# Two decoder stages share TensorE: where the media key and value projections stand, how the first statistics are issued, and how the media sums begin

## The chip, the cores and the metric

The kernel runs on one core of a Trainium2 chip. A core has a TensorE for matrix products (its weight loads are shown apart in the profile, as PEld), a VectorE (DVE), a ScalarE (ACT) and a GpSimd (POOL), which run their own queues in order and wait for each other by semaphores. SyncE (SP) issues most of the transfers, which sixteen DMA engines carry out. Matrix products land in PSUM, which VectorE, ScalarE and others empty.

The metric is the device time of one launch in microseconds (us). One execution of the kernel was taken with the hardware profiler; the trace and the page of profile come from it.

## The reference, cut to what matters

A decoder of two layers works on `x`, 8 rows of 512 tokens with 256 channels, in six residual stages, each behind a layer norm. The change touches the fourth and the fifth, `L1_attn` and `L1_xattn`.

The fourth is an attention in integers. Each `quant_act` needs the largest magnitude of its whole tensor before the first value can be rounded:

```python
def quant_act(x, bit):
    n = 2 ** (bit - 1) - 1
    s = jnp.max(jnp.abs(x)) / n
    xq = jnp.clip(ste_round(x / s), -n - 1, n)
    return (xq * s, s)
...
aw = jnp.einsum('ntd,nsd->nts', q, k)
aw, aws = quant_act(aw, 8)
probs, ps = int_softmax(aw, aws, 8)
probs, ps = quant_act(probs, 8)
attn = jnp.einsum('nts,nsd->ntd', probs, v)
attn, as_ = quant_act(attn, 8)
attn = attn.transpose(1, 0, 2).reshape(T, B, E)
out, _ = quant_linear(attn, as_, wo, bo)
```

It has 16 heads of 16 channels and attends over the batch of 8, at each of the 512 positions. So its matrices are small, and many of them are laid out together.

The fifth attends from `x` to a second input, the context or media (`ctx`, also 8 x 512 x 256). Its keys and values depend on the context and a weight alone, and not on anything that the earlier stages compute:

```python
q = xn @ Wq * scale
kv = media @ Wkv
k, v = jnp.split(kv, 2, axis=-1)
...
sim = jnp.einsum('bhid,bhjd->bhij', q, k)
sim = jnp.where(media_mask[:, None, None, :], sim, neg_inf)
attn = jax.nn.softmax(sim, axis=-1)
out = jnp.einsum('bhij,bhjd->bhid', attn, v)
return out @ Wout
```

Here `xn` is `x` behind two layer norms, and there are 8 heads of 64 channels. A mixture of experts (`L1_ffn`) follows and ends the program.

## The kernel before, in words

The class `FastDecoder` keeps `x` in SBUF as 32 tiles of 128 tokens and runs the stages one after the other. A layer on top of the language places the instructions on the queues: each engine's order follows the order of the program, corrected by priorities. `tc.high_priority(AT_ONCE)` moves what is issued under it ahead of other work that is ready; `tc.issue_after(i)` keeps it behind an instruction `i`; `newest(engine)` is the last instruction issued so far for an engine.

**The media keys and values** are computed ahead, wherever TensorE has room in the integer attention. `keys_values` (L2742) takes rows of the context; for each it makes eight *groups*, four of the keys and four of the values. A group is two fp32 products of 128 x 512 (L2773, two records each in the trace, so four records), one copy from PSUM by ScalarE into one of three `kv_o` tiles (L2778), and one transfer of 256 KB to DRAM on SP (L2779). The media stage later loads `ma_kT` and `ma_v` from there (1 MB each, L2860).

**The integer attention** (`stage_quantized_attention`, L2404) runs through five pools of tiles:

- qa1 quantizes `x` and computes queries, keys and values; row 0 of the media keys and values is made here.
- qa2 computes the scores (TensorE, L2590 and L2596) and reduces them (VectorE).
- qa3 is the integer softmax (L2784), nearly all VectorE. Beside it `keys_values` makes rows 1 to 5. Their five contexts are loaded at once into `room`, a tile of the tag `qa_big` with room for eight.
- qa4 is the loop over the values, `for n in range(9)`. `spread(n)` copies the values of step n into a tile with zeros between the heads, two of four copies on GpSimd and two on VectorE (L2631, 1.15 us each). `turn(n)` rounds the probabilities (VectorE), widens them with four ScalarE operations (L2641), transposes them in two halves on TensorE (L2649), and copies each half out on VectorE (L2652). `weigh(n - 1)` does the products (L2662), one ScalarE copy into `m_[:, n - 1]` (L2670) and one VectorE reduction for the largest magnitude (L2671). After each step two groups of rows 6 and 7 follow, 16 in all, from a generator: `keys_values(range(6, B), None, "tr", 4)`. With `room` None, the context of each row has the tile `kv_ctx`, of which there is one buffer. The groups take their PSUM from the same four `tr` buffers as the transposes. `m_`, 8 x 1024 values on each partition, is a new tile of the tag `qa_big`.
- Behind the loop the magnitudes are reduced to one number over all partitions, and a few one-column VectorE operations make the scales. `bias_parts` (L2383) splits the output bias into three bf16 pieces with ten VectorE operations, and one more scales a row (`orow`).
- qa5 rounds `m_` in eight pieces (ScalarE L2709, then VectorE L2710), transposes them (TensorE, L2713) and copies the result out through a helper that shares the copies between VectorE and ScalarE (L101, L103). Then, for each of the 8 rows of x, the output product (L2726, L2729) fills one of two PSUM buffers `pj`, VectorE multiplies it by the scale (L2731), and the sum is added to `x` (L2733), on GpSimd for rows 2, 4 and 6 and on VectorE otherwise. After row 0, `twice_normal` (L3014) computes the statistics that the media stage's first row needs: four `bn_stats`, and small operations on 128 x 4 values, most in two reciprocal square roots of ten operations each (L1477 to L1481).

**The media stage** (`stage_media_attention`, L2835) loads keys and values of a row, normalizes it, and works through eight steps for each row: scores of two key tiles (L2901, two PSUM buffers), two exponentials on ScalarE (L2907, into four buffers `ma_e`), the products with the values (L2925), and a running sum of the four exponentials of each pair of heads. The sum begins with a copy of the first exponential by GpSimd (L2912); the three others are added by VectorE (L2914). The softmax is divided by these sums at the end.

Of the kernel before, what the change touches and what calls it, by code (L numbers as in the profile page):

```python
# [27 lines left out]
F32 = mybir.dt.float32  # L28
# [6 lines left out]
ALU = mybir.AluOpType  # L35
# [4 lines left out]
P = 128  # L40
B, S, C = 8, 512, 256
NST = S // P
# [1235 lines left out]
class FastDecoder(Decoder):  # L1278
# [1125 lines left out]
    def stage_quantized_attention(self, w):  # L2404
        nc, q = self.nc, self.q
        wT, ident, ones, magic = q["wT"], q["ident"], q["ones"], q["magic"]
        tc = self.tc
        with tc.tile_pool(reuse_waits="tile", name="qa", bufs=1) as pool:
# [195 lines left out]
            with tc.tile_pool(reuse_waits="tile", name="qa3", bufs=2) as tmp, tc.tile_pool(  # L2604
                reuse_waits="tile", name="qp3", bufs=4, space=PSUM
            ) as psum:
                ptop = self.integer_softmax(tmp, aw, qs, atop)
                room = self.alloc(pool, [P, 8, 2, S], F32, "qa_big")
                for _ in self.keys_values(tmp, psum, range(1, 6), room, "kv", 4):
                    pass  # L2610

                ps_, _ = self.scaled(pool, ptop, 1.0 / 128.0 / 127.0, "qa_ps")
                pr = one("qa_pr")
                nc.vector.reciprocal(pr, ptop)
                nc.vector.tensor_scalar(pr, pr, 127.0, None, ALU.mult)


            m_ = self.alloc(pool, [P, 8, 4, C], F32, "qa_big")
            mtops = one("qa_mtops", 8)

            vz = h16("vz").rearrange("p (j i m a r d) -> p j i m a r d", j=2, i=NST, m=4, a=4, r=4)
# [1 line left out]
            with tc.tile_pool(reuse_waits="tile", name="qa4", bufs=2) as tmp, tc.tile_pool(  # L2623
# [48 lines left out]
                        mtops[:, n : n + 1], m_[:, n], AX.XY, ALU.max, apply_absolute_value=True  # L2672
                    )

                ahead = self.keys_values(tmp, psum, range(6, B), None, "tr", 4)
                for n in range(9):
                    if n < 8:
                        spread(n)
                        turn(n)
                    if n:  # L2680
                        weigh(n - 1)
                    for _ in range(2):
                        next(ahead, None)


            mtop = one("qa_mpart")
            nc.vector.tensor_reduce(mtop, mtops, AX.X, ALU.max)
# [7 lines left out]
            nc.vector.reciprocal(osc_inv, osc)  # L2695
            mT = h16("mT").rearrange("p (c i t m) -> p c i t m", c=2, i=NST, t=B)
            brow = self.alloc(pool, [P, C], BF16, "qa_orow")
            self.bias_parts(brow, q["rb"][:, 3 * C :], osc_inv, "qa_b")
            with tc.tile_pool(reuse_waits="tile", name="qa5", bufs=2) as tmp, tc.tile_pool(
                reuse_waits="tile", name="qp5", bufs=1, space=PSUM  # L2700
            ) as psum:
                orow = self.alloc(tmp, [P, C], F32, "qa_orow_s", bufs=1)
                nc.vector.tensor_scalar(orow, q["wsc"][:, C:], osc, None, ALU.mult)
                for n in range(0, 8, 2):
                    ps = [self.alloc(psum, [P, 8, P], BF16, "tr", bufs=4) for c in range(2)]
                    for h in range(2):
                        f = m_[:, n + h]
                        mi = self.alloc(tmp, [P, 4, C], BF16, "qa_mi")
                        nc.scalar.activation(f, f, AF.Identity, bias=magic[:, 0:1], scale=mr)  # L2709
                        nc.vector.tensor_scalar(mi, f, -MAGIC, None, ALU.add)  # L2710
                        for c in range(2):
                            for m in range(4):
                                nc.tensor.transpose(  # L2713
                                    ps[c][:, 4 * h + m], mi[:, m, c * P : (c + 1) * P], ident
                                )
                    for c in range(2):
                        for st in range(NST):
                            self.evac(
                                mT[:, c, st, :, 16 * n : 16 * n + 32].rearrange("p t (m k) -> p t m k", k=4),
                                ps[c][:, :, 32 * st : 32 * st + 32].rearrange("p m (k t) -> p t m k", t=B),  # L2720
                            )
                for b in range(B):
                    ps = self.alloc(psum, [P, NST, C], F32, "pj", bufs=2)
                    for st in range(NST):
                        for c in range(2):
                            nc.tensor.matmul(  # L2726
                                ps[:, st], mT[:, c, st, b], wT[:, c, 3 * C :], start=(c == 0), stop=False
                            )
                        nc.tensor.matmul(ps[:, st], ones[:, :P], brow, start=False, stop=True)  # L2729
                    o = self.alloc(tmp, [P, NST, C], F32, "qa_o")  # L2730
                    nc.vector.tensor_tensor(o, ps, orow.unsqueeze(1).broadcast_to([P, NST, C]), ALU.mult)  # L2731
                    x = self.x[:, b * NST : (b + 1) * NST, :]
                    (nc.gpsimd if b in (2, 4, 6) else nc.vector).tensor_tensor(x, x, o, ALU.add)  # L2733
                    if b == 0:
                        self.media_stats = {b: self.twice_normal(tmp, b, self.const)}
        self.integers.close()

    def load_media_attention(self):
        self.w_media = super().load_media_attention()
        return self.w_media  # L2740

    def keys_values(self, pool, psum, rows, room, tag, bufs, outs=None):  # L2742

# [91 lines left out]
    def stage_media_attention(self, w, out):  # L2835


        nc, t = self.nc, self.t
        wq, wkv, wo = w
        later = Background()  # L2840
        with self.tc.tile_pool(reuse_waits="tile", name="ma", bufs=2) as pool, self.tc.tile_pool(
# [50 lines left out]
            def scores(n):  # L2892
# [12 lines left out]
                for kt, ps in zip(kts, both):  # L2905
# [1 line left out]
                    nc.scalar.activation(  # L2907
                        ex, ps, AF.Exp, bias=bias[:, b * NST + kt : b * NST + kt + 1], scale=0.125
                    )
                    if kt == 0:  # L2910
                        d["sum", c] = self.alloc(pool, [P, 2, 512], F32, "ma_esum", bufs=3)
                        nc.gpsimd.tensor_copy(d["sum", c], ex)  # L2912
                    else:
                        nc.vector.tensor_tensor(d["sum", c], d["sum", c], ex, ALU.add)  # L2914

            def weigh(n):
                b, rest = divmod(n, 8)
# [622 lines left out]
```

## Time and profile before

| | |
|---|---|
| three runs | 3056.48, 3062.92 and 3061.24 us; median 3061.24 us |
| profiled execution | 3056.84 us, its span in the trace 3054.9 us |
| granted TensorE clock, mean over the span | 0.970 of full speed |
| TensorE | busy 2839.3 us, 93% of the span |
| VectorE | busy 2063.4 us, 68% |
| ScalarE | busy 1192.1 us, 39% |
| GpSimd | busy 428.7 us, 14% |

The trace says where the stages of interest lie (us from the start of the span; busy times from the table of windows over these stretches):

| stage | from, to | TensorE busy | VectorE busy | ScalarE busy | granted clock |
|---|---|---|---|---|---|
| scores and before | 2110 to 2190 | 62.6 of 80 | 59.5 | 24.8 | 0.87 |
| integer softmax, rows 1 to 5 of keys and values | 2190 to 2258 | 61.3 of 68 | 65.4 | 35.9 | 0.97 |
| values loop, rows 6 and 7 | 2258 to 2311 | 45.5 of 53 | 34.8 | 37.5 | 0.91 |
| largest magnitude, rounding, transposes | 2311 to 2329.5 | 10.9 of 18.5 | 15.0 | 14.1 | 0.54 |
| output, first media statistics | 2329.5 to 2353.7 | 11.7 of 24.2 | 23.2 | 0.0 | 0.77 |
| media attention | 2353.7 to 2790 | 421.7 of 436.3 | 313.6 | 174.2 | 0.98 |
| experts, to the end | 2790 to 3054.9 | 237.3 of 264.9 | 36.8 | 40.8 | 0.93 |

How to read what follows: a row of the table of windows gives a stretch of time and what each engine was busy in it, with the number of instructions in brackets. A row of the timeline gives the start, the length, the engine, the line, the operation, the tiles it writes and reads and their shapes, and in square brackets how long the engine had been idle before it and what ended that wait. "x8" at the end of a row means that eight neighbouring records are merged into one. An engine's idle time costs nothing where another engine sets the pace.

### The profile page before, as it was taken

The numbers are of one execution on the slowest core, as the hardware profiler recorded it, in microseconds if no ns is written. First come the engines' busy times: TensorE is split into PE (matmuls) and PEld (weight loads), VectorE is DVE, ScalarE is ACT, GpSimd is POOL, SyncE is SP. The second block draws the span as 40 slices with busy tenths as digits, with TensorE's granted clock in tenths as the row PEclk, the third lists the DMA queues.
The fourth block names the chain that finished last, engine by engine and source line by source line (L and its number), as shares of the span: only waits on it lengthen the run. The fifth ranks groups of instructions, "written<-read, shape, count | busy, mean of one in ns | idle before, by whom it ended". The sixth has DMA issues, their size and how long they took to land. (4 is left out here: it accounts for less than half of the span.)

```text
span 3054.9 us, 39805 instructions
## 1 busy us (share of the span) xinstructions
PE 2839.3 (93%) x14929; PEld 1513.9 (50%) x14944; DVE 2063.4 (68%) x4546; ACT 1192.1 (39%) x1687; POOL 428.7 (14%) x389
## 2 busy tenths in 40 slices
PE   8999999979999999999999999999786999997998
PEld 5653333225555556555555556555344344444665
DVE  7458999977776784356776788548788876764110
ACT  2237776744444421134445421115363444441111
POOL 1111111100011010000011011112111123331111
PEclk9999999988999999999999999999897999997999
DMA  7001212101000011001000012010332132314231
GB/s 245 1 35 51 70 51 68 38 14 57 16 22 22 16 31 36 1 1 43 16 22 22 16 46 69 14 42 28 122 123 82 43 105 76 112 50 104 101 139 62
DMA packets 130695, 168.72 MB, mean 55 GB/s; under 512 B 51761, under 2 KB 79666, under 8 KB 128443
## 3 DMA queue, kind: packets, MB, share of 16 engines
q1 hardware_dynamic: 126394, 154.48, 15.9%
q0 software_dynamic: 4096, 11.59, 1.0%
q8 instruction: 119, 1.95, 0.3%
q14 instruction: 86, 0.70, 0.1%
HBM read 113.12 MB, written 47.50 MB: 53 GB/s over the span
## 5 line engine op out<-in xcount | busy, mean ns | idle before, releaser
L1889 PE MATMUL pj<-w,la_hT 128*128 128x512 f32 x720 | 333.3, 603 | 5.2 <-ACT la_qkT L1942 4.5
L1736 DVE TENSOR_TENSOR x_e<-x_e,x_share 128x1024 f32<-128x1024 f32 x256 | 315.8, 1276 | 14.3 <-ACT x_e L1735 14.2
L1735 ACT ACTIVATE x_e<-sc 128x1024 f32<-128x1024 f32 x256 | 249.3, 1023 | 82.9 <-PE sc L1724 82.9
L1889 PEld LDWEIGHTS pj<-w,la_hT 128*128 128x128 f32 x720 | 132.2, 191 | 152.7 <-issue 113.7
L2016 DVE TENSOR_TENSOR la_e<-sc,la_mask 128x1024 f32<-128x1024 f32 (+1 forms) x128 | 135.3, 1083 | 103.8 <-PE sc L2007 103.8
L3283 POOL TENSOR_TENSOR la_oT<-la_o,x_wide 128x512 f32<-128x512 f32 x64 | 97.9, 1541 | 753.0 <-DMA x_wide<-invs 647.9
L2907 ACT ACTIVATE ma_e<-sc,ma_bias 128x1024 f32<-128x1024 f32 x128 | 135.6, 1110 | 147.3 <-PE sc L2901 145.8
L2233 ACT ACTIVATE lf_gate<-pj,lf_b 128x512 f32<-128x512 f32 (+1 forms) x82 | 56.3, 687 | 334.5 <-PE pj L2212 322.6
L2020 ACT ACTIVATE la_e<-la_e 128x1024 f32<-128x1024 f32 (+1 forms) x128 | 117.5, 946 | 151.8 <-DVE la_e L2016 150.7
L2212 PE MATMUL pj<-lf_hnT,w 128*128 128x512 f32 (+1 forms) x368 | 171.3, 593 | 2.8 <-DVE lf_hid L2238 2.8
L1752 PE MATMUL po<-x_e,x_v 128*32 128x512 f32 x1024 | 139.8, 618 | 34.1 <-DVE x_e L1736 30.1
L2914 DVE TENSOR_TENSOR ma_esum<-ma_esum,ma_e 128x1024 f32<-128x1024 f32 x96 | 120.6, 1260 | 58.8 <-ACT ma_e L2907 30.0
L2212 PE MATMUL sc<-lf_hnT,w 128*128 128x512 f32 x336 | 157.7, 592 | 0.0
L1724 PE MATMUL sc<-x_q,x_k 32*128 32x512 f32 x1024 | 152.5, 645 | 1.7 <-DVE sa_ok L1448 1.4
L2284 PE MATMUL po<-w,lf_hid 128*128 128x256 f32 x640 | 149.0, 379 | 0.0
L2238 DVE SCALAR_TENSOR_TENSOR lf_hid<-sc,lf_b,lf_gate 128x512 f32<-128x512 f32 x70 | 52.4, 748 | 136.9 <-PE sc L2212 133.8
L2027 PE MATMUL po<-la_e,la_v 128*64 128x256 f32 (+1 forms) x1024 | 125.2, 369 | 6.7 <-ACT la_o L2044 6.0
L2007 PE MATMUL sc<-la_qkT 64*128 64x256 f32 (+1 forms) x1024 | 128.9, 375 | 1.1 <-DVE la_e L2016 0.6
L2284 PEld LDWEIGHTS po<-w,lf_hid 128*128 128x128 f32 x640 | 117.8, 190 | 21.2 <-issue 7.4
L2901 PE MATMUL sc<-ma_qT,ma_kT 64*128 64x512 f32 x512 | 127.3, 615 | 0.4 <-ACT ma_e L2907 0.4
L2925 PE MATMUL po<-ma_e,ma_v 128*64 128x512 f32 x512 | 125.2, 610 | 0.0
L2070 PE MATMUL pj<-w,la_oT 128*128 128x256 f32 x512 | 121.0, 383 | 2.0 <-DVE lf_t L1480 0.7
(493 smaller groups left out, 5206.8 us busy)
## 6 DMA issues: line engine op xcount, KB each, us to landing
x_wide<-invs SPq DMA_DIRECT2D x184, 128.0 KB
w<-in_f_w_dram SPq DMA_DIRECT2D x16, 1024.0 KB
kv<-kv_o SPq DMA_DIRECT2D x56, 256.0 KB
slots<-x_empty SPq DMA_DIRECT2D x8, 1028.0 KB
x_mask<-in_x_maskT_dram SPq DMA_DIRECT2D x8, 1024.0 KB
ma_kT<-kv SPq DMA_DIRECT2D x8, 1024.0 KB
ma_v<-kv SPq DMA_DIRECT2D x8, 1024.0 KB
ex_rows<-slots SPq DMA_DIRECT2D x7, 1028.0 KB
```

The costliest lines, as they stand in the source:

```text
L1724: nc.tensor.matmul(pair[r // 2][:, r % 2, :], d["k"][rows, g, kt * P : (kt + 1) * P], d["q"][rows, e, g, :], start=True, stop=True,)
L1735: nc.scalar.activation(ex, d["e"][rest][p], AF.Exp)
L1736: nc.vector.tensor_tensor(ex, ex, d["share"][:, kt, :].unsqueeze(1).broadcast_to([P, 2, 512]), ALU.mult)
L1752: nc.tensor.matmul(d["po"][32 * r : 32 * r + 32, :], d["v"][:, kt, 8 * g + 2 * r + e, :], ex[r // 2][:, r % 2, :], start=(kt == 0), stop=( ...
L1889: nc.tensor.matmul(ps, d["hT"][:, k, i * P : (i + 1) * P], wqkv[:, k, j * S : (j + 1) * S], start=(k == 0), stop=(k == 1),)
L2007: nc.tensor.matmul(both[half][:, r, jj * 256 : jj * 256 + to - j * P], d["qkT"][rows, 4 + c, j * P : (j + 1) * P], d["qkT"][rows, c, j * P ...
L2016: nc.vector.tensor_tensor(ex[:, :, :n_cols], ps[:, :, :n_cols], mask[:, :n_cols].unsqueeze(1).broadcast_to([P, 2, n_cols]), ALU.add,)
L2027: nc.tensor.matmul(out[:, j * P : to], lhsT(j), ex[:, jj * 256 : jj * 256 + to - j * P], start=(j == 0), stop=(j == 3), skip_group_check=True,
L2212: nc.tensor.matmul(ps[:m, :], w1[:, k, at : at + m], held[b]["hnT"][:, k, :], start=(k == 0), stop=(k == 1))
L2284: nc.tensor.matmul(ps[:, :C], held[b]["hid"][:, f, i * P : (i + 1) * P], w2[:, f, :], start=(f == 0), stop=False,)
L2901: nc.tensor.matmul(both[m // 2][:, r, :], d["k"][rows, c, kt * P : (kt + 1) * P], d["q"][rows, c, :], start=True, stop=True,)
L2907: nc.scalar.activation(ex, ps, AF.Exp, bias=bias[:, b * NST + kt : b * NST + kt + 1], scale=0.125)
```

## The change

It has four parts.

1. **The 16 groups of rows 6 and 7 are spread.** `context` loads one context and `keys_values_group` makes one group; `project(tmp, psum, tag, count)` takes the next `count` groups from a list. Three are issued in the softmax, behind the forty of rows 1 to 5. In the values loop one follows each step except where n % 4 is 3, that is seven, and two more behind the loop. One is issued behind each output product until the list is empty, which takes the last four (rows 0 to 3 of x). The context of row 6 now has a place in `room`; that of row 7 has a tile of its own in a new pool `qx`. `m_` is no longer a new tile but a view of `room`.
2. **The bias rows are moved**: `bias_parts` and the scaling of `orow` are issued behind the second pair of rounded pieces (n == 2) and no longer ahead of the first.
3. **The first media statistics are unbroken**: they are issued at the highest priority, and the product and the sum of every row of x after the first (`o` and `x`) are kept behind their last VectorE instruction.
4. **The media sums begin as a sum of two**: nothing is done for the first exponential (kt == 0); the second step adds the first two exponentials into the sum's tile. The GpSimd copies are gone.

In the changed kernel each engine's queue is then ordered as follows where it differs. On TensorE one group stands ahead of a step's transposes in the loop, three behind the last weighing, and in the output two half groups and then whole ones alternate with the products of rows 0 to 3. On ScalarE three `kv_o` copies stand ahead of the first widening, and two stand between the first copies of the rounding. On VectorE the statistics follow the first row of x without a gap. On SP the context of row 7 stands behind three `kv_o` writes, and the loads of `ma_kT` and `ma_v` for the first media row behind the last write.

```diff
                 for _ in self.keys_values(tmp, psum, range(1, 6), room, "kv", 4):
                     pass
 
+                ctx6 = self.context(room[:, 5], 6)
+                groups = [(ctx6, 6, j, g) for j in range(2) for g in range(NST)]
+
+                def project(tmp, psum, tag, count=1):
+                    for group in groups[:count]:
+                        self.keys_values_group(tmp, psum, *group, tag, 4)
+                    del groups[:count]
+
+                project(tmp, psum, "kv", 3)
...
-            m_ = self.alloc(pool, [P, 8, 4, C], F32, "qa_big")
+            m_ = room.rearrange("p n a s -> p n (a s)").rearrange("p n (m c) -> p n m c", c=C)
+            stay = ExitStack()
+            late = stay.enter_context(tc.tile_pool(reuse_waits="tile", name="qx", bufs=1))
+            ctx7 = self.context(self.alloc(late, [P, 2, S], F32, "qa_ctx"), 7)
+            groups += [(ctx7, 7, j, g) for j in range(2) for g in range(NST)]
...
-                ahead = self.keys_values(tmp, psum, range(6, B), None, "tr", 4)
                 for n in range(9):
                     if n < 8:
                         spread(n)
                         turn(n)
                     if n:
                         weigh(n - 1)
-                    for _ in range(2):
-                        next(ahead, None)
-
+                    if n % 4 != 3:
+                        project(tmp, psum, "tr")
+                project(tmp, psum, "tr", 2)
...
-            self.bias_parts(brow, q["rb"][:, 3 * C :], osc_inv, "qa_b")
...
-                nc.vector.tensor_scalar(orow, q["wsc"][:, C:], osc, None, ALU.mult)
...
+                    if n == 2:
+                        self.bias_parts(brow, q["rb"][:, 3 * C :], osc_inv, "qa_b")
+                        nc.vector.tensor_scalar(orow, q["wsc"][:, C:], osc, None, ALU.mult)
                 for b in range(B):
...
+                    project(tmp, psum, "tr")
                     o = self.alloc(tmp, [P, NST, C], F32, "qa_o")
-                    nc.vector.tensor_tensor(o, ps, orow.unsqueeze(1).broadcast_to([P, NST, C]), ALU.mult)
                     x = self.x[:, b * NST : (b + 1) * NST, :]
-                    (nc.gpsimd if b in (2, 4, 6) else nc.vector).tensor_tensor(x, x, o, ALU.add)
+                    with self.tc.issue_after(ahead) if b else nullcontext():
+                        nc.vector.tensor_tensor(o, ps, orow.unsqueeze(1).broadcast_to([P, NST, C]), ALU.mult)
+                        (nc.gpsimd if b in (2, 4, 6) else nc.vector).tensor_tensor(x, x, o, ALU.add)
                     if b == 0:
-                        self.media_stats = {b: self.twice_normal(tmp, b, self.const)}
+                        with self.tc.high_priority(self.AT_ONCE):
+                            self.media_stats = {b: self.twice_normal(tmp, b, self.const)}
+                        ahead = self.newest(mybir.EngineType.DVE)
+            stay.close()
...
+    def context(self, out, b):
+        self.nc.sync.dma_start(
+            out, self.t["ctxT"].rearrange("(k p) n -> p k n", p=P)[:, :, b * S : (b + 1) * S]
+        )
+        return out
+
+    def keys_values_group(self, pool, psum, ctxT, b, j, g, tag, bufs):
+        nc, wkv = self.nc, self.w_media[1]
+        ps = self.alloc(psum, [P, 1, S], F32, tag, bufs=bufs)
+        at = slice(g * P, (g + 1) * P)
+        for k in range(2):
+            w, x = wkv[:, k, j * S : (j + 1) * S], ctxT[:, k, :]
+            w, x = (w[:, at], x) if j == 0 else (x[:, at], w)
+            nc.tensor.matmul(ps[:, 0], w, x, start=(k == 0), stop=(k == 1))
+        o = self.alloc(pool, [P, 1, S], F32, "kv_o", bufs=3)
+        nc.scalar.copy(o, ps)
+        nc.sync.dma_start(self.kv[b, j][:, g * S : (g + 1) * S], o.rearrange("p a n -> p (a n)"))
...
-                    if kt == 0:
+                    if kt == 1:
                         d["sum", c] = self.alloc(pool, [P, 2, 512], F32, "ma_esum", bufs=3)
-                        nc.gpsimd.tensor_copy(d["sum", c], ex)
-                    else:
-                        nc.vector.tensor_tensor(d["sum", c], d["sum", c], ex, ALU.add)
+                    if kt:
+                        nc.vector.tensor_tensor(d["sum", c], d[4 * c] if kt == 1 else d["sum", c], ex, ALU.add)
```

## The prediction, made before the changed kernel ran

> **What bounds the kernel now.** I read the page first (TensorE busy 93% of a 3054.9 us span), then found where the changed lines run, and read the table of windows from 2258 us on; in each row the numbers are length, busy time of TensorE, its weight loads, VectorE, ScalarE and GpSimd, granted TensorE clock, DMA share and GB/s:
>
> ```profile
> 2258.00:2310.00 52.00, 45.53 (x704) 25.93 (x704) 34.41 (x38) 37.52 (x54) 12.89 (x12) 0.91 0.27 93
> 2310.00:2330.00 20.00, 11.43 (x87) 9.01 (x88) 15.85 (x43) 14.14 (x24) 0.35 (x1) 0.57 0.42 159
> 2330.00:2350.00 20.00, 11.19 (x75) 8.46 (x73) 19.64 (x30) 0.00 (x0) 8.05 (x5) 0.81 0.16 52
> 2368.00:2468.00 100.00, 97.72 (x424) 37.62 (x420) 78.37 (x242) 46.56 (x51) 20.38 (x17) 1.00 0.20 65
> ```
>
> So there are four stages with four limits. The values loop (first row) is TensorE's: 45.5 of 52 us. Rounding the values (second) is shared by VectorE and ScalarE. The output (third) is VectorE's, 19.6 of 20. Media attention (fourth) is TensorE's again. Next came the timeline of VectorE in the values loop (start, length, line, idle time before it and its releaser):
>
> ```profile
> 2266.48 1.29 DVE L2652 COPY qa_pT<-tr 128x1024 bf16<-128x1024 bf16 x2 [4.80 <-PE tr L2649]
> 2267.80 2.31 DVE L2631 COPY qa_h<-qa_h 32x1024 bf16<-32x1024 bf16 x2
> 2270.14 1.22 DVE L2671 TENSOR_REDUCE qa_mtops<-qa_big 128x1 f32<-128x1024 f32 x1
> 2271.62 1.29 DVE L2652 COPY qa_pT<-tr 128x1024 bf16<-128x1024 bf16 x2 [0.27 <-PE tr L2649]
> ...
> 2292.51 1.29 DVE L2652 COPY qa_pT<-tr 128x1024 bf16<-128x1024 bf16 x2 [5.65 <-PE tr L2649]
> ...
> 2308.92 1.22 DVE L2671 TENSOR_REDUCE qa_mtops<-qa_big 128x1 f32<-128x1024 f32 x1 [3.03 <-ACT qa_big L2670]
> ```
>
> The period is 5.14 us (2266.48 to 2271.62), and VectorE fills 4.87 of it: it is only 0.27 behind TensorE. The other idle pieces are large: 4.80, 5.65, 0.86 and 3.03. TensorE's own timeline says why:
>
> ```profile
> 2259.06 1.89 PE L2649 MATMUL tr<-qw_ident,qa_wide 128*128 128x128 bf16 x16 [7.73 <-ACT qa_wide L2641]
> 2260.74 5.26 PE L2773 MATMUL tr<-kv_ctx,w 128*128 128x512 f32 x8
> ...
> 2272.58 3.70 PE L2773 MATMUL tr<-w,kv_ctx 128*128 128x512 f32 x8
> ...
> 2286.65 5.37 PE L2773 MATMUL tr<-kv_ctx,w 128*128 128x512 f32 x8 [3.20 <-DMA kv_ctx<-in_ctxT_dram]
> ```
>
> Two projection groups are 8 records: 3.43 us from start to start when warm. They take 5.26 after 7.73 us of idleness, and 5.37 after the 3.20 us wait for a context that has one buffer.
>
> **Projections spread (16 groups of rows 6 and 7).** The work is the same: per group 4 matmul records (1.72 us warm), one ScalarE copy (0.58) and one 256 KB write on SP. Before, all 16 stood in the values loop; now 3 stand in the softmax, 9 in the loop (3 of them behind its last weighing), 4 in the output.
>
> *Softmax, 3 groups.* The 40 groups there end at 2251.3 and TensorE idles to 2259.06, so 5.15 us fit, to 2256.5. But their copies stand before the first widening on ScalarE's queue: the third ends near 2256.5 + 0.06 + 0.58 = 2257.14, where the widening started at 2256.08. Loss 1.06. TensorE's gap shrinks to 2260.12 - 2256.5 = 3.6 us. A gap of 3.20 cooled it above, so I take a cold start again. Row 6's context load joins five at 2175.67, last in the queue: 0 (up to 0.5).
>
> *Loop start.* Cold transposes 1.89, then one group instead of two: cold to about 4.8 us after the restart, as before, so it ends near 2265.1. Transposes 1.0 and weighing 0.6 follow, and the first spread copy (2267.80) starts near 2267.1: gain 0.7, 1.06 already taken off. A warm start would give 2.7.
>
> *Six full turns.* TensorE now needs 1.0 + 0.6 + 1.72 = 3.3, ScalarE 4 x 0.74 + 0.99 + 0.58 = 4.5, VectorE 1.29 + 2.31 + 1.22 = 4.82, with gaps 4.88. VectorE is next: six turns are 29.3, two last reductions 2.44, the last weighing and its copy 0.7. That is 32.4, against 2310.14 - 2267.80 = 42.3. Gain 9.9. The context wait goes, since row 7 has its own tile, loaded near 2257.8 behind three writes on SP and read some 30 us later.
>
> *The clock.* The thinned loop leaves gaps of 1.5 us in a turn with a group, 3.2 in the two without. The trace's nearest row is the scores stage (L2590), also limited by VectorE:
>
> ```profile
> 2160.00:2165.00 5.00, 2.98 (x151) 1.66 (x140) 3.70 (x3) 0.00 (x0) 1.46 (x1) 1.00 0.24 53
> 2165.00:2170.00 5.00, 2.89 (x156) 1.63 (x157) 3.92 (x3) 0.00 (x0) 5.00 (x1) 0.84 0.01 3
> 2170.00:2175.00 5.00, 3.54 (x215) 2.00 (x192) 4.44 (x5) 0.00 (x0) 4.58 (x5) 0.50 0.01 3
> ```
>
> At 60% busy and with gaps of at most 1.9 us the clock held 1.00 for a while, then fell to 0.50. The Trainium skill, "TensorE: Matmul & The Clock Gate", section "HAM oscillation — how this bites in real kernels", speaks of gaps over about 3.4 us only: by the rule the loop stays warm and loses 0. By the row a turn with a group may run cold: 1.89 + 0.7 + 3.43 = 6.0 against 4.88, so 1.1 each, 5.7 if all five behind the start are cold. A cold TensorE is then busy all the time, which warmed it in 5 us above. I take one such turn, 1.1; ends 0 and 5.7. The loop gives 0.7 + 9.9 - 1.1 = **9.5**.
>
> **Behind the loop.** Three groups (5.2 us) run while the maximum is reduced; before, the first rounded tile came 7.7 us after the last weighing. Moving the bias rows (eleven VectorE instructions, 4.0 us) behind the first rounded tiles brings that to 4.7. But VectorE's total is unchanged: 4.0 + 8 x 0.69 + 16 x 0.36 = 15.3 of the 16.5 us that it took from 2311.5 to 2328.0. ScalarE's 14.1 gain two copies (1.2) in the middle. Both come out at the same place: 0 (-1 to +1).
>
> **Output and statistics.** From the first product (2329.58) to the first normalized tile of media (2353.71) it took 24.1. Now: product and sum 2.3; four statistics 1.7; 27 small instructions that depend on each other, at 0.195 (17 of them fill 2350.36 to 2353.67), 5.3; then seven products and four sums at 1.14, 12.5. Sum 21.8. Behind the statistics wait, by the new order, those products, GpSimd's three sums (2.35 each), and TensorE's fourth row, whose two PSUM buffers are full; the four groups fill its queue meanwhile, to about 8 us, and the fourth row starts near 10.3. Against it stands the contention of two engines:
>
> ```profile
> 2337.95 1.36 DVE L148 COPY ma_ln_mean<-ma_ln_mv 128x4 f32<-128x4 f32 x1
> ...
> 2347.70 1.32 DVE L1480 TENSOR_TENSOR ma_ln_t<-ma_ln_t,ma_ln_var 128x4 f32<-128x4 f32 x1
> ```
>
> Both should take 0.16; each ends with a GpSimd sum. "GPSIMD Engine Reference", section "1. Specifications", says the SBUF interfaces are shared, with contention for VectorE instructions with two SBUF inputs. Unbroken, the small ones escape, but VectorE's sums have two SBUF inputs and now stand beside GpSimd's. By the row, only the last sum is held, 1.2; by the rule, all three may be, 3.5. I take 2.0: 23.8, gain **0.3** (-2.7 to +1.3). Media's key loads stood on SP at 2309.68; now they stand behind the last write, some 8 us into the output, still near 30 us before the scores (2366.96) need them. Two MB at the 300 GB/s of that time take 7 us: 0.
>
> **Media's sums.** 32 GpSimd copies (1.04 each) go; 96 VectorE additions stay, the first now of two exponentials. VectorE waited 25.9 us for those copies in ten places, but TensorE is busy 97.7 of 100 us here and waited for the additions 2.4 + 1.8. So most of it is hidden anyway: gain **1.2** (0 to 4).
>
> **Sum.** 9.5 + 0 + 0.3 + 1.2 = 11.0. The profiled execution took 3056.84 (span 3054.9 and 1.9 around it), so it becomes 3045.8. The median of the three runs, 3061.24, is 4.4 higher; the same gain there gives **3050**.
>
> **Rivals.** *Cold loop:* the five turns stay cold and the output loses: 11.0 - 4.6 - 3.0 = 3.4, near 3057.8. For it: the clock of 0.50 above. Against: a saturated TensorE rewarms. *Hidden anyway:* VectorE, only 0.27 behind, holds the period, which is true, but the 5.65, the 3.03 and half of the start are waits and not periods. Kept without them: six turns at 0.27 and media, some 3 us, near 3058. *Slower, by one mechanism:* the first exponential's buffer in media (four of them) was freed by GpSimd's copy; now VectorE's addition, which also needs the second exponential, frees it, about 1.1 us or more later, and VectorE is 78% busy. If ScalarE then starts an exponential late, TensorE stops. It decides when each of the 32 sums costs over 11.0/32 = 0.34 us; at 0.5 it is 3061.2 + 16 - 11.0, near 3066. Against it: ScalarE's exponentials waited 145.8 us for TensorE and 1.5 for VectorE, and the buffer comes round two steps, some 8 us, later.
>
> **How the numbers follow.** Main case 0.72: 3050, own range 3043 to 3055. Cold loop 0.12, hidden anyway 0.06, slower 0.10. What a measurement tells from no change is 0.2%, 6.1 us, so "same" lies between 3055.1 and 3067.4. The main case is faster but for its tail (0.70 and 0.02); the two middle rivals, 3057.8 and 3058, are "same" (0.18); the slower one, whose 3066 lies just inside and whose price may well be higher, counts as slower in 0.08 and as same in 0.02. Faster 0.70, same 0.22, slower 0.08. The range leaves the slow case and the best ends out: 3042 to 3060; 3042 is a warm start (2.0) and media's best with runs 3 us below the median.
>
> **What would show it.** Right: the turns of the loop at 4.9 us with no idle VectorE; no wait for a context; last reduction near 2300; first media tile 10 us earlier; no GpSimd copy in media. Wrong: turns at 6 us at clock 0.5; over 25 us from first product to first media tile; ScalarE's exponentials waiting for VectorE.

## The result, and the profile after

Six runs of the changed kernel have a median of 3034.36 us (3032.32 to 3041.64), six of the kernel before 3057.8 us (3050.19 to 3062.92). The ratio is 0.9937 with a 95% interval of 0.9923 to 0.9951: faster by 0.5 to 0.8%, 15 to 24 us, where 11 were forecast. The median lies below the forecast range (3042 to 3060, with 3050 in the middle). Of the 15.6 us between 3050 and the median, 3.4 are the level of the kernel before, which the forecast took as 3061.24 from three runs; the rest is the gain. The profiled execution took 3039.56 us against 3056.84 (17.3 less) with a span of 3037.8. These are rows of the table of windows of the changed kernel for the values loop, the rounding, the output and 100 us of media (columns as before):

```profile
2257.00:2293.00 36.00, 30.14 (x671) 19.09 (x672) 27.85 (x40) 32.85 (x46) 12.75 (x13) 0.91 0.20 68
2293.00:2316.00 23.00, 13.96 (x85) 8.84 (x84) 14.77 (x40) 15.40 (x26) 0.32 (x1) 0.63 0.09 35
2316.00:2345.00 29.00, 17.63 (x100) 11.50 (x98) 21.04 (x48) 2.34 (x4) 10.28 (x6) 0.91 0.50 182
2359.00:2459.00 100.00, 99.34 (x430) 38.27 (x426) 76.07 (x250) 46.95 (x52) 10.44 (x8) 1.00 0.20 65
```

The row of the loop fell from 52 us to 36. Those of rounding and output, 20 and 20 before, became 23 and 29: VectorE was busy for 19.6 of 20 us in the output and now for 21.0 of 29. TensorE is busy 99.3 of 100 us in media, and was 97.7. To place the gain exactly I follow six events through the profiles; each stage runs from one to the next (us). The forecast of the loop alone is 9.9 less 1.1 for a cold turn.

| stage | before | changed | won | forecast |
|---|---|---|---|---|
| up to the first spread copy on VectorE in the loop | 2267.80 | 2266.66 | 1.1 | 0.7 |
| loop: to the end of the last reduction | 42.37 | 25.98 | 16.4 | 8.8 |
| rounding: to VectorE's first output product | 19.41 | 23.70 | -4.3 | 0 |
| output: to the first normalized media tile | 24.13 | 28.83 | -4.7 | 0.3 |
| to the first media scores | 13.25 | 12.89 | 0.4 | 0 |
| media: to the end of the last output projection | 417.98 | 409.04 | 8.9 | 1.2 |
| experts, to the end | 269.96 | 270.70 | -0.7 | 0 |

The sum is 17.1, the difference of the spans. Four terms were far off, and their errors partly cancel. Only the lengths of stages can be compared over different profiles: with the same instructions ahead of it, the loop began at 2267.80 in the kernel before, at 2269.73 in the first experiment and at 2256.56 in the eighth. That is more than most of these terms, so the 1.1 of the first row is no measure of the change. The stages of one kernel, though, repeated within 0.1 us (the changed kernel again: 25.99, 23.71, 28.83, 12.90, 409.00).

### The profile page after: what moved, and what is told of

It reads as the page before. It is cut to its first block, busy times and chain, and to the rows that moved or that the text cites. A ratio compares the mean times of both kernels' runs of the same rounds, so it can differ in the third digit from the quotient of the medians.

```text
span 3037.8 us, 39774 instructions
## 1 busy us (share of the span) xinstructions
PE 2832.6 (93%) x14929; PEld 1511.4 (50%) x14944; DVE 2039.3 (67%) x4546; ACT 1191.5 (39%) x1687; POOL 388.1 (13%) x357
## 5 line engine op out<-in xcount | busy, mean ns | idle before, releaser
L1736 DVE TENSOR_TENSOR x_e<-x_e,x_share 128x1024 f32<-128x1024 f32 x256 | 315.9, 1277 | 14.3 <-ACT x_e L1735 14.1
L3320 POOL TENSOR_TENSOR la_oT<-la_o,x_wide 128x512 f32<-128x512 f32 x64 | 97.7, 1538 | 753.1 <-DMA x_wide<-invs 678.6
L2284 PEld LDWEIGHTS po<-w,lf_hid 128*128 128x128 f32 x640 | 117.8, 190 | 21.2 <-issue 7.4
L1905 DVE TENSOR_REDUCE la_ss<-la_sq 128x16 f32<-128x1024 f32 x64 | 77.7, 1215 | 65.8 <-ACT la_sq L1896 65.8
```

Source lines behind the costliest of these rows:

```text
L1736: nc.vector.tensor_tensor(ex, ex, d["share"][:, kt, :].unsqueeze(1).broadcast_to([P, 2, 512]), ALU.mult)
L2284: nc.tensor.matmul(ps[:, :C], held[b]["hid"][:, f, i * P : (i + 1) * P], w2[:, f, :], start=(f == 0), stop=False,)
```

## The experiments

The table gives the stages of each run as above. What was expected of a run stands behind its edit, and what came of it behind that.

| run | loop | rounding | output | media |
|---|---|---|---|---|
| e1, media sums alone | 42.23 | 19.39 | 24.13 | 409.35 |
| e2, projections spread alone | 26.46 | 23.17 | 26.19 | 419.73 |
| e3, statistics as before | 26.60 | 22.74 | 26.18 | 409.30 |
| e4, bias rows first | 26.66 | 22.87 | 28.83 | 408.15 |
| e5, tail groups to the output | 25.97 | 19.08 | 26.67 | 409.50 |
| e6, eight places for the products | 26.76 | 22.57 | 22.70 | 408.54 |
| e7, GpSimd kept busy | 30.80 | 24.25 | 28.81 | 409.18 |
| e8, before, spread on VectorE | 42.53 | 19.89 | 24.39 | 419.83 |
| e9, e5 and e6 together | 26.46 | 18.23 | 25.19 | 409.06 |
| e11, e9 with the bias rows first | 26.52 | 19.50 | 23.97 | 409.45 |
| e12, GpSimd half busy | 26.71 | 22.74 | 28.82 | 409.41 |
| e13, VectorE's copies repeated | 39.46 | 23.05 | 28.81 | 408.96 |
| e14, spread on VectorE | 29.12 | 24.31 | 28.82 | 409.09 |

### e1 and e2: one part of the change alone

e1 is the kernel before with the last hunk of the change only; e2 has the first hunks, of softmax, loop and output. The core of each:

```diff
-                    if kt == 0:
+                    if kt == 1:
                         d["sum", c] = self.alloc(pool, [P, 2, 512], F32, "ma_esum", bufs=3)
-                        nc.gpsimd.tensor_copy(d["sum", c], ex)
...
-                ahead = self.keys_values(tmp, psum, range(6, B), None, "tr", 4)
...
+                    if n % 4 != 3:
+                        project(tmp, psum, "tr")
+                project(tmp, psum, "tr", 2)
...
+                    project(tmp, psum, "tr")
                     o = self.alloc(tmp, [P, NST, C], F32, "qa_o")
```

> The kernel before with part 4 alone (media sums begin as a sum of two). The stage runs from the first media scores to the last output projection: 418.0 us before, 409.0 in the changed kernel. Theory: the whole difference comes from the sums, because GpSimd's copy made the additions late and TensorE's sum products waited, part of it hidden inside their busy time; the stage takes 409 +-1 and the profiled execution is near 3048. Rival (my forecast): only the idle time that the rows show is won, 1.2 us: stage 416.8, execution near 3055.6, and the rest of the 9 us belongs to the other parts of the change.

> The kernel before with part 1 alone (projections spread, row 7's own context, m_ as a view); bias rows ahead of the rounding, statistics and media sums as before. Theory: the loop gives its 17.5 us in full (last reduction near 2292.6), rounding (last reduction to first product, 19.4 before, 23.7 changed) still loses some 2 us because ScalarE's copies and TensorE's half group stand in its queues, output (first product to first normalized media tile, 24.1 before, 28.8 changed) stays near 24, media stays at 418: execution near 3042. Rival: the loop's extra 8 us need the other parts too (then the last reduction is near 2300, as forecast), or rounding loses 4 us whatever stands with the bias rows (then it is the groups alone).

e1 took 3048.3 us in the median, 0.9956 of the kernel before (0.9936 to 0.9977). Media fell to 409.35, so 8.6 of the 8.9 us belong to the sums alone; the rival falls. (Over all profiles the stage took 417.98 to 419.83 in the three with the old sums and 408.15 to 409.50 in the thirteen with the new ones.) Why my 1.2 was too small is seen in TensorE's timeline of the sum products. First the kernel before, then e1:

```profile
2539.73 1.06 PE L2944 MATMUL sum<-ma_esum,ones 128*32 128x512 f32 x8
2563.17 1.05 PE L2944 MATMUL sum<-ma_esum,ones 128*32 128x512 f32 x4
2564.47 1.05 PE L2944 MATMUL sum<-ma_esum,ones 128*32 128x512 f32 x4 [0.25 <-DVE ma_esum L2914]
```

```profile
2562.95 1.07 PE L2943 MATMUL sum<-ma_esum,ones 128*32 128x512 f32 x8
```

Eight records take 1.06 us when all are ready, and so do four. Where the second sum came late, in five of fourteen places, the eight fell in two halves of 1.05, and only the gap between them (0.25 here, up to 0.67) counts as idle. In the groups by line the same 112 records of the same mean length were busy longer:

```profile
L2944 PE MATMUL sum<-ma_esum,ones 128*32 128x512 f32 x112 | 20.1, 605 | 2.4 <-DVE ma_esum L2914 2.4
```

```profile
L2981 PE MATMUL sum<-ma_esum,ones 128*32 128x512 f32 x112 | 15.3, 605 | 0.0
```

The first row is the kernel before, the second the changed one: 4.8 of busy time and 2.4 of idle time go, 7.2 in all; smaller waits at other products make up the rest. Why the additions came late is known in part. In all five places the one that released the late half took 1.87 us in place of 1.22, beside a GpSimd copy for the next sums (1.54 to 1.96 in place of 1.04). That is 0.65 of the 1.3 to 1.7 us lost in each place. How much of the rest came through waiting for an earlier copy was not separated.

e2 took 0.9958 (0.9938 to 0.9977). The loop's gain needs no other part. But rounding lost its 4 us although the bias rows stood where they had been, as the rival had it, and the output lost 2.1 without the new order of the statistics, where it had been expected to stay near 24.

### e3 to e6: rounding and output

The edits of e3, e4, e5 and e6, in this order, each to the changed kernel:

```diff
-                    with self.tc.issue_after(ahead) if b else nullcontext():
...
-                        with self.tc.high_priority(self.AT_ONCE):
-                            self.media_stats = {b: self.twice_normal(tmp, b, self.const)}
+                        self.media_stats = {b: self.twice_normal(tmp, b, self.const)}
...
             brow = self.alloc(pool, [P, C], BF16, "qa_orow")
+            self.bias_parts(brow, q["rb"][:, 3 * C :], osc_inv, "qa_b")
...
-                    if n == 2:
-                        self.bias_parts(brow, q["rb"][:, 3 * C :], osc_inv, "qa_b")
...
-                    if n % 4 != 3:
+                    if n % 4 != 3 and n < 8:
                         project(tmp, psum, "tr")
-                project(tmp, psum, "tr", 2)
...
-                    o = self.alloc(tmp, [P, NST, C], F32, "qa_o")
+                    o = m_[:, b]
```

> The changed kernel without part 3: the statistics are issued without priority and the products of later rows are not held behind them. Theory: the small statistics used to fill VectorE's waits for GpSimd's sums; unbroken they leave three empty waits of 2.2 us. So the output stage goes from 28.8 back to about 24 to 25 us and the execution falls by 4 to 5. Rival: the stage is long because the four groups stand between the products on TensorE's queue; then it stays near 28.

> The changed kernel with the bias rows back ahead of the rounding (part 2 undone). Theory: behind the second pair the bias rows' tile waits for a transfer of a kv_o tile (1.9 us on VectorE) and the eleven operations stand between the rounded pieces, so undoing it brings rounding from 23.7 to about 21. Rival: the three groups behind the loop and the half group ahead of the first product make the loss, and rounding stays at 23.7 or gets longer by up to 2.

> The changed kernel, but none of the groups stands behind the last weighing: those three go to the output, which then has seven, one behind each of the products of rows 0 to 6. Theory: with three groups behind the loop, ScalarE's queue gets seven (changed) or eight (part 1 alone) of the eight roundings ahead of the first copy-out of transposed pieces, six before; here it is four. So rounding (last reduction to first product) returns from 23.7 to 19.4 or less, 18 to 19.5. Rival: the eleven bias operations between the rounded pieces are what keeps it long, and it stays above 22; the output, with three groups more on TensorE, gets at most 1 longer, as TensorE waits there.

> The changed kernel with the eight output products in eight places (the rows of m_, free by then) and not in two buffers. Theory: VectorE's product of row 3, 5 and 7 waits for GpSimd's sum of row 2, 4, 6 to free its buffer, 2.2 us each; with eight places these waits go and the output (28.8) is 2.5 + 6.7 + 7 products and 4 sums at 1.2 = 22.4 to 24. Rival: it is TensorE's two PSUM buffers or the contention with GpSimd that holds VectorE; then the output stays above 26 and VectorE's own products get longer than 1.25.

**Rounding.** Moving the bias rows back gave 0.8 (e4), where 2.7 had been expected; taking the three groups away gave 4.6 (e5). ScalarE's timeline shows how, first of e2, then of e5:

```profile
2290.59 1.24 ACT L2722 ACTIVATE qa_big<-qa_big,qw_magic,qa_mr 128x1024 f32<-128x1024 f32 x1 [0.90 <-DVE qa_mr L2704]
2291.74 0.56 ACT L2773 COPY kv_o<-tr 128x512 f32<-128x512 f32 x1
2292.20 1.24 ACT L2722 ACTIVATE qa_big<-qa_big,qw_magic,qa_mr 128x1024 f32<-128x1024 f32 x1
2293.35 0.57 ACT L2773 COPY kv_o<-tr 128x512 f32<-128x512 f32 x1
2293.81 6.90 ACT L2722 ACTIVATE qa_big<-qa_big,qw_magic,qa_mr 128x1024 f32<-128x1024 f32 x6
2300.62 0.62 ACT L101 COPY qa_h<-tr 128x256 bf16<-128x256 bf16 x2
```

```profile
2297.33 4.63 ACT L2719 ACTIVATE qa_big<-qa_big,qw_magic,qa_mr 128x1024 f32<-128x1024 f32 x4 [2.39 <-DVE qa_mr L2703]
2301.88 0.61 ACT L101 COPY qa_h<-tr 128x256 bf16<-128x256 bf16 x2
```

In e2 all eight roundings and two copies of groups stand ahead of the first copy-out of transposed pieces, 10.0 us after the first rounding; in e5 four roundings, 4.6 us. The kernel before had six there. VectorE's share of the copies stands behind ScalarE's first one: in e2 VectorE waited 4.05 us for it, with the later rounded pieces behind on its own queue:

```profile
2301.00 0.42 DVE L103 COPY qa_h<-tr 128x256 bf16<-128x256 bf16 x1 [4.05 <-ACT qa_h L101]
```

So the groups cost little by their own length (two copies, 1.1): their presence changed the order that was laid out for ScalarE's queue. e5 also takes half a group on TensorE from ahead of the first output product. VectorE waited 2.66 us for that product in the changed kernel and 2.10 in e5, so this is at most 0.6 of the 4.6. The order alone, with the groups in place, was not tried.

**Output.** e3 gives 26.18 instead of 28.83: the statistics' new order cost 2.65, where 4 to 5 had been expected. It is e2's figure, so part 1 accounts for the other 2.05. In e3 three small operations of VectorE stood for 2.35, 2.34 and 1.19 us beside GpSimd's sums, in the kernel before for 1.36, 0.89 and 1.32; this is 2.3 more, about the size of it. VectorE's timeline of the changed kernel shows what the small operations had filled:

```profile
2325.59 2.36 DVE L2748 TENSOR_TENSOR qa_o<-pj,qa_orow_s 128x1024 f32<-128x1024 f32 x2
2327.86 1.22 DVE L2749 TENSOR_TENSOR x<-x,qa_o 128x1024 f32<-128x1024 f32 x1
2331.31 2.36 DVE L2748 TENSOR_TENSOR qa_o<-pj,qa_orow_s 128x1024 f32<-128x1024 f32 x2 [2.23 <-POOL x L2749]
2333.58 1.22 DVE L2749 TENSOR_TENSOR x<-x,qa_o 128x1024 f32<-128x1024 f32 x1
2337.03 2.36 DVE L2748 TENSOR_TENSOR qa_o<-pj,qa_orow_s 128x1024 f32<-128x1024 f32 x2 [2.24 <-PE pj L2743]
```

Two products, one sum, then 2.23 idle, three times: the product of the next row needs one of two `qa_o` buffers, and GpSimd's sum holds it. (The second wait is put down to TensorE, whose product was itself held by the same buffers.) e6 takes the limit away, and the output falls to 22.70; no wait is left but the 1.5 for the first product, ahead of the stage. In e5 the output fell too, to 26.67, though it had three groups more: one wait of 2.23 was left there, and GpSimd's second and third sums began before VectorE's next ones, which then took 2.35 each.

### e7, e8, e12, e13 and e14: the length of the spread copies

In the changed kernel VectorE's two spread copies of a turn got shorter and shorter; the first, third and fourth turn:

```profile
2266.66 2.25 DVE L2645 COPY qa_h<-qa_h 32x1024 bf16<-32x1024 bf16 x2
...
2275.18 1.02 DVE L2645 COPY qa_h<-qa_h 32x1024 bf16<-32x1024 bf16 x2
...
2278.80 0.87 DVE L2645 COPY qa_h<-qa_h 32x1024 bf16<-32x1024 bf16 x2
```

Before, VectorE came to its copies 0.1 to 0.4 us behind GpSimd in every turn, and they took 2.1 to 2.4; over six turns that is 13.8 us before and 7.2 changed. These are GpSimd's copies, in the kernel before (where VectorE's began at 2267.80), then in the first, third and fourth turn of the changed kernel; the one at 2275.80 is for the fourth:

```profile
2267.62 2.20 POOL L2631 COPY qa_h<-qa_h 32x1024 bf16<-32x1024 bf16 x2 [12.66 <-PE po L2662]
```

```profile
2266.42 2.20 POOL L2645 COPY qa_h<-qa_h 32x1024 bf16<-32x1024 bf16 x2 [12.15 <-PE po L2676]
...
2273.34 2.12 POOL L2645 COPY qa_h<-qa_h 32x1024 bf16<-32x1024 bf16 x2 [1.38 <-PE po L2676]
2275.80 2.38 POOL L2645 COPY qa_h<-qa_h 32x1024 bf16<-32x1024 bf16 x2 [0.34 <-PE po L2676]
```

GpSimd starts as soon as TensorE has released the tile. VectorE, with other work ahead on its queue, came 1.5 to 3.0 us later from the second turn on, when GpSimd's copies were nearly or wholly done. The edits: e7 and e12 add, behind GpSimd's copies, four or two copies of half a row into a scratch tile; e8 (of the kernel before) and e14 (of the changed one) put VectorE for GpSimd in `spread`; e13 repeats VectorE's copies. In the order e7 (e12 has `range(2)`), e8 and e14, e13:

```diff
+                    for r in range(4):
+                        rows_ = slice(32 * (r % 2), 32 * (r % 2) + 32)
+                        nc.gpsimd.tensor_copy(
+                            extra[rows_].rearrange("p (i a d) -> p i a d", a=4, d=16),
...
-                        (nc.gpsimd if r < 2 else nc.vector).tensor_copy(
+                        nc.vector.tensor_copy(
...
-                    for r in range(4):
+                    for r in (0, 1, 2, 3, 2, 3, 2):
```

> The changed kernel with more GpSimd work in the values loop: behind its two spread copies of each step it copies half of each again, four copies of 32 x 512, into a scratch tile that nothing reads. Theory: VectorE's spread copies take 0.43 us each where GpSimd is idle and 1.15 beside a GpSimd copy, so with GpSimd busy for 4 us of each turn they are back at about 1.1, 2.2 to 2.3 a turn, the turns go from about 4.2 to 4.9, and the loop (first spread copy to last reduction) from 26.0 to about 31 or 32. Rival: the copies got shorter for another reason (less traffic, a thinner TensorE queue); they stay at 0.43 and the loop at 26.

> The kernel before with all four spread copies of a step on VectorE, none on GpSimd. Theory: alone, a copy takes 0.43 us, so four take 1.75 and less than the two beside GpSimd did (2.31); VectorE has 4.3 us of work in a turn, but TensorE sets the turn at 5.0, so the loop (42.4) falls by 1 at most: contention cost nothing as long as the 16 groups stood in the loop. Rival: the copies take 1.15 each also without GpSimd; then VectorE has 7.1 us a turn and the loop gets longer by about 13.

> As the run with GpSimd kept busy, with half of the added work: two copies of 32 x 512 in each step, 1.35 us, so that GpSimd has 3.5 us of work in a turn of 4.2 and can't set the pace itself. Theory: VectorE's twelve spread copies, 7.2 us in all in the changed kernel, 13.8 in the one before and 10.1 with four added copies, come to 8 to 10 us, and the loop (26.0) grows by no more than their growth, since ScalarE has 4.2 of work in a turn. Rival: the loop grows by over 4 as before, so it was GpSimd's queue and not VectorE's copies; or the copies stay at 7.2.

> The changed kernel with VectorE's two spread copies of each step repeated (the same values written again to the same place): five copies of 0.44 and not two, 2.2 us a turn, as much as the forecast had for two beside GpSimd (2.31). Theory: the forecast of the loop (32.4 from the first spread copy to the last reduction, at 4.88 a turn set by VectorE) failed on this one term; with the term put back the turns take 4.7 to 5.0 and the loop 29.5 to 32.5, against 26.0. Rival: ScalarE sets the turn at 4.2 with room to spare on VectorE, and the length of the copies didn't matter; then the loop stays at 26 to 27.5.

> The changed kernel with all four spread copies of each step on VectorE. Theory: four alone take 1.76 a turn, so VectorE has 1.29 + 1.76 + 1.22 = 4.3 a turn, just over ScalarE's 4.2, and GpSimd nothing: the loop is 26 to 27.5, that is GpSimd's help is worth about nothing here. Rival: copies get longer beside ScalarE and TensorE in the thin loop as well (0.6 or more each), and the loop goes to 28 or more.

e8 settles the duration: without GpSimd four copies take 1.76, 0.44 each, less than two beside it. It also shows that this was worth nothing while 16 groups stood in the loop (42.53).

```profile
2261.70 1.76 DVE L2631 COPY qa_h<-qa_h 32x1024 bf16<-32x1024 bf16 x4
```

e7 and e12 do not settle the price: in e7 the copies grew by 2.9 us in all and the loop by 4.8, since GpSimd was busy 28.0 of 30.8 us and set the turn itself; in e12 the copies grew by 1.7 and the loop by 0.7. e13 and e14 load VectorE directly. In e14 its spread copies take 10.5 us in the six turns, 3.3 more, and the loop is 3.1 longer; in e13 21.2 us, 14.0 more, and the loop is 13.5 longer. Both missed the size that I had expected, e13 as its repeated copies ran beside GpSimd again, e14 as I had left ScalarE's 4.2 us a turn as cover. In these two each us of copies cost 0.94 to 0.96 us of the loop, and VectorE set the pace there. These are the windows of the loop in the changed kernel and in e13 (columns as in the result):

```profile
2266.66:2292.64 25.98, 22.27 (x570) 13.96 (x569) 23.95 (x33) 23.57 (x33) 12.48 (x12) 1.00 0.15 55
```

```profile
2262.82:2302.28 39.46, 27.22 (x572) 16.59 (x571) 37.85 (x51) 24.72 (x34) 12.55 (x12) 0.87 0.11 41
```

TensorE's clock was lower in e13 (0.87), but that is not what made its loop long: VectorE's waits there sum to 0.35 us (to 1.2 in e14). In the changed kernel VectorE's waits sum to 1.5 us, so the first us of added copies can be cheaper, as in e12. ScalarE did not wait there at all from 2264.6 to 2287.8, and the last three turns, from one weighing to the next, took 4.20 each, the length of ScalarE's work. So with the shorter copies VectorE no longer sets the pace alone.

### e9 to e11: mended

> The changed kernel with the edits of two earlier runs together: no group behind the last weighing (three more in the output) and eight places for the output products. If the two losses are separate, they add: rounding 19.1 (23.7), output near 22.7 (28.8), loop, media and experts as in the changed kernel; together 10.7 us less, execution 0.35% below the changed kernel on the same chip and near 3027 in a profile that starts alike. Rival: with seven groups in the output and no wait for GpSimd, TensorE's queue becomes what holds the products there, and the output stays at 25 or more; then only 7 to 8 are won.

> The changed kernel as it is, again, beside the other runs on this chip: 0.993 to 0.994 of the kernel before, the loop 26, rounding 23.7, output 28.8, media 409.

> The run before with both losses mended, and the bias rows ahead of the rounding again. Theory: in the changed kernel the bias rows cost 0.8 (23.70 against 22.87) where they stood, mostly as they waited 1.9 for a transfer; without groups behind the loop nothing is left to wait for, and their place is worth 0 +-0.7: rounding 18.5 to 20. Rival: ahead of the rounding they are on the path as they were in the kernel before, and rounding gets over 1 longer than with the bias late.

On one chip e9 took 3032.05 us in the median and the changed kernel 3039.61; against the kernel before 0.9908 (0.9888 to 0.9928) and 0.9941 (0.9921 to 0.9960). The intervals overlap a little, so in times the version is only probably better than the change. In stages it won 5.5 in rounding and 3.6 in output. The output is not the 22.7 of e6. The rival had this number (25 or more), but not its cause: VectorE did not wait for TensorE within the stage. VectorE and GpSimd show what happened (the same three microseconds of both):

```profile
2320.99 2.35 DVE L2748 TENSOR_TENSOR x<-x,qa_big 128x1024 f32<-128x1024 f32 x1
```

```profile
2319.90 2.35 POOL L2748 TENSOR_TENSOR x<-x,qa_big 128x1024 f32<-128x1024 f32 x1 [2.30 <-DVE qa_big L2747]
```

GpSimd's sum began first and kept its 2.35; VectorE's sum, 1.22 alone, ended 1.1 after it. In e6 VectorE mostly began first, and it was GpSimd whose sums took 3.26. e11 has 1.3 more in rounding and 1.2 less in output than e9: the bias rows' late place is a gain of 1.3 once no group stands behind the loop, as the rival had it, and in their stages, over one profile of e11, the two versions come out level.

## Why the prediction was wrong in size

- **Loop, 9.5 forecast, 17.5 measured, with the start in both.** The step that failed is the term 2.31 in "VectorE 1.29 + 2.31 + 1.22 = 4.82". I took the duration of the spread copies from rows in which they began just behind GpSimd's, and kept it for a loop in which VectorE comes to them later. The term is 13.8 us for six turns and measured 7.2. With it fell the statement that VectorE is next: turns forecast at 4.88 took 2.4 to 3.4 at first, while ScalarE was ahead, and then ScalarE's 4.20 (I had 4.5 for it). What the 6.6 us of copies were worth is an estimate between the runs: 5.8 on the line from e12 to e13, 6.3 on the line from e14 to e13. The cold turn charged with 1.1 did not come. Both together are 6.9 to 7.4 of the 7.5 that lie between 33.5 (32.4 and the cold turn) and the measured 26.0. The other 0.4 lay in the start, and is less than the starts differ from profile to profile.
- **Clock.** The cold start was forecast rightly: the first 16 transposes took 1.89 after 3.55 us of idleness, the next two sets 1.35 and 1.06. Behind it no gap of TensorE in the loop was longer than 1.1, and the granted clock was 1.00 to its end. So the scores stage, where the clock fell with gaps of up to 1.9, was no model for the loop. The rule of the Trainium skill ("TensorE: Matmul & The Clock Gate", section "HAM oscillation — how this bites in real kernels"), which names gaps over about 3.4 us, gave the right answer here, but shorter gaps were not safe in these runs: the granted clock fell to 0.50 within a gap of 2.74 us in the rounding of the changed kernel, and within one of 2.43 in e13's loop.
- **Rounding, 0 forecast, -4.3 measured.** The step that failed is "ScalarE's 14.1 gain two copies (1.2) in the middle. Both come out at the same place". It counted the copies by their length; with the three groups behind the loop, seven of eight roundings and not six stood ahead of ScalarE's first copy-out (four in e5, which is 4.6 shorter). The order of the eight roundings against the copy-outs was on the queues to be read before the run; I had read only where the groups' copies stood. Moving the bias rows did not bring what it was credited with while groups stood behind the loop: VectorE's first bias operation waited 1.94 us there for a transfer.
- **Output, 0.3 forecast, -4.7 measured.** The failed step is "seven products and four sums at 1.14, 12.5". The statistics ahead of them came as forecast (9.3 from the first product on); then the products and sums took 19.6. The step let them run without a gap, and 6.7 of this are three waits. I had named the two PSUM buffers, but not the two `qa_o` buffers that GpSimd's sums hold; the broken-up statistics had been the filling of those waits. The 2.0 for contention was charged to VectorE, and it was GpSimd's sum that got longer (3.25 for 2.35), which lengthened the waits.
- **Media, 1.2 forecast, 8.9 measured.** The failed step is "TensorE is busy 97.7 of 100 us here and waited for the additions 2.4 + 1.8. So most of it is hidden anyway". It took busy time for work. 4.8 us of it was products that ran as four records where eight take no longer.
- **The rivals.** The loop did not stay cold, and the gain was not hidden. The slower case found its waits, though not its price: in media ScalarE's exponentials now wait 3.7 us in two places for VectorE's sums, and TensorE waits for an exponential 0.4 as before.

## What to carry to other kernels

A duration from a row holds for its neighbourhood: before a VectorE copy is carried into a new schedule, ask what GpSimd was doing beside it, and look for the same shape without it. In a matrix stage count a late operand by the halves into which it splits the products too, not only by the idle time. When broken-up small work is gathered, look what waits it had filled, and follow every buffer count, in SBUF as in PSUM.

## What was new about the hardware

VectorE and GpSimd did not slow each other down side by side: in these operations one waited for the other to end. VectorE's bf16 copies took 0.42 alone and about 1.15 when they began just behind a GpSimd copy; of two fp32 sums from SBUF the one that began first kept its time (GpSimd's 2.35 or VectorE's 1.22) and the other ended 1.1 us or 2.2 us behind it (VectorE's in 2.35, GpSimd's in 3.25). VectorE's reductions beside GpSimd stayed at 1.22. The Trainium skill, "SBUF — State Buffer", section "Who interferes with whom", describes an exclusive lock on a shared pair of ports, held for a whole instruction, which copies in their two-port modes need and reductions on this chip do not, and says that operations with two SBUF inputs contend with GpSimd's reads; these rows agree with it. Read beside the loop's rows, it would have said to ask when VectorE comes to its copies, which is what the failed term left out.
